# A four-layer graph network: the first stage's roots moved to ScalarE, its mask taken from bytes, its statistics summed unmerged, and an eighth of every third difference tile on GpSimd

## The chip, the core and the metric

The kernel runs on one core of a Trainium2 chip. The metric is device microseconds (us) of one execution; of several executions the median counts. The engines are PE (TensorE matmul, with PEld for its weight loads), DVE (VectorE), ACT (ScalarE), POOL (GpSimd) and SP (SyncE, which issues most DMAs here).

## The reference, cut to what matters

128 graphs of 128 nodes with 128 features pass four residual layers. The change lies in the first stage of the kernel, which computes layer 0 and the first half of layer 1:

```python
def _layernorm(x, axis=-1, eps=1e-5): ...        # (x - mean) / sqrt(var + eps)
# layer 0: relations 1 to 7; adj holds only 0 and 1 here, so one relation has edges
h = jnp.maximum(_layernorm(x), 0.0)
mask = (adj == r); degree = clip(mask.sum(axis=2), 1e-06)
agg = agg + einsum('bts,bsd->btd', mask / degree, h) @ rel_weights[r]
out = agg + h @ self_w.T + self_b
x = x + relu(layernorm(out) * ln_gamma + ln_beta)
# layer 1
h = jnp.maximum(_layernorm(x), 0.0)
D = jnp.abs(h[:, :, None, :] - h[:, None, :, :])
z = einsum('bijc,oc->bijo', D, W1) + b1           # 64 outputs for every pair i, j
m = mean(z over b, i, j); v = mean((z - m) ** 2 over b, i, j)
z = leaky((z - m) / sqrt(v + EPS) * g1 + be1)     # needs m and v of all 128 graphs
...
```

The mean and the variance of `z` over all pairs of all graphs stand between the first stage and the second.

## The kernel before, in words

There are three stages, one after the other, in one program. The first, `two_stages` up to line 755, computes layer 0 and `z`, writes `z` to memory in HBM and collects its statistics. After a short step that folds the statistics (lines 758 to 797), the second stage reads `z` back and finishes layer 1. The third computes layers 2 and 3. The change touches the first stage and the fold.

**Tiles of the first stage.** `z` is symmetric in i and j, so only half of the pairs are computed: for every graph b, 64 shifts of the node index, in 4 tiles of 2 x 8 shifts. That makes 512 tiles, numbered i = 4b + t, each 128 features by 2048 pairs. One tile passes four engines:

- `difference` (line 317): subtracts shifted features (`xe`, in SBUF) from the own ones. Tiles t = 1 and 3 (`ON_POOL`) run on GpSimd, t = 0 and 2 on VectorE, where the second operand is the copy in PSUM (`XP`). The tile t = 0 takes a maximum in place of the difference, with a correction by TensorE.
- `absolute` (line 375): ScalarE, in place, for t = 1, 2, 3.
- `products` (line 332): TensorE, 4 matmuls with `w1T` for t > 0, and 8 for t = 0.
- `evacuate` (line 345): ScalarE copies the result from PSUM into `z`, 128 x 1024.
- `statistics` (line 361): VectorE, two or three `bn_stats` for each tile. After every fourth graph `bn_aggr` (lines 372, 373) merges these into two means and variances for the group, in `ST1`.
- `kept` (line 357): SP stores `z`.

**Layer 0.** `chain(g)` (line 427) handles a group of G = 4 graphs, 32 groups in all, while the tiles of an earlier group run. Its three layer norms (of x, of layer 0's output `o`, and of the new x) each take `moments` on VectorE (lines 450, 452), and then `roots` (line 454) on GpSimd: an addition, a power of -0.5 (`rsqrt`, lines 231, 232) and `shift` (lines 289, 290), which forms -mean/deviation. ScalarE then applies them, in `centred` (line 473, four instructions of 128 x 128 for `hn`, four for `o`) and `h1` (line 514). `masked` (line 460) compares the integer adjacency with 1 on GpSimd, `degree` (464) sums it on VectorE, `shared` (477) divides on GpSimd; `m8` (537) keeps the adjacency as bytes for later layers. TensorE turns and multiplies (483 to 497), `joined` (500) adds the bias on VectorE from PSUM, `scaled` (504, 505) applies gamma and beta, `ended` (508) the relu and the residual.

**What sets the order.** Each piece of work is a `step`: a name, an engine, a cost in us, the steps that it needs, a rank. `_ranked` (line 109) plays these costs through, with one in-order queue for each engine, and always takes the step that can begin earliest; among those that begin within `NEAR` of each other, the lowest rank goes first. `RANK1` shifts the ranks by name. The result is one fixed order for each engine, written out before the program is built. `TAKEN` says which step holds one of the two PSUM tiles `sm` until which other step has read it.

A second copy of the first two stages, `two_stages(True)`, is in the program for other data; it is not executed with these inputs.

Of the kernel before, what the change touches and what calls it, by code (L numbers as in the profile page):

```python
# [17 lines left out]
P = 128  # L18
G = 4
# [11 lines left out]
ON_POOL = {1, 3}  # L31
BY_MAX = 0
# [7 lines left out]
HOPS, DEEP, ARRIVING, NEAR = 0.1, 0.25, 2.4, 0.025  # L40
LATE = {"SP": 0.0, "Pool": 0.02, "ACT": 0.1, "DVE": 0.08, "PE": 0.1}
RANK1 = {"small": 5.5, "on_all": -21, "selfb": -88.5, "both_t": 69.5, "fold": 22.5, "zero": 86.5, "xp": (25, 6.5),
         "xe": (-73.5, 2), "again": (30.5, -38), "pw": (38, -59), "xw": (84, 10.5), "load": 14, "mask": 8.5,
         "mv": 80.5, "deg": -48, "rs": -7, "most": -70, "per": 38.5, "hn": 21.5, "share": -74.5, "pt": 14,
         "hT": -24, "pm": -81.5, "maskT": 22.5, "ph": 19, "hw": 36, "m8": -10.5, "po": -82, "o": 88, "mvo": 36,
         "rso": -75.5, "oc": -23.5, "on": 62, "end": -58.5, "x": -53, "mvx": 54.5, "rsx": -54.5,
         "h1": (-13, -93.5),
         "d": (48.5, 10, -31.5, -34.5, -16.5, -63, -6, 36, 58.5, -27, -180, -50, -73.5, -31, 64, -37.5),
         "hp": (72.5, -76.5, 26, -8, 34.5, -30, -54, 43.5, 18.5, -53, 1, 6.5, -22, -157, -120, 31),
         "hs": (-114.5, -49, 10.5, -47, 55, -49, -39, -106, -123, 81, -8, -22, -42, -6.5, 17, -105),  # L50
         "st": (-5, 6.5, -4, -3.5, -137.5, -143, 69, -12.5, 117, -194.5, -100, 126, -35, -10.5, -62.5, 20.5),
         "abs": (-29.5, 55.5, -114, 8, 2, 59.5, -12.5, 6, -22, 21.5, 3.5, -62.5),
         "out0": (-10.5, -14, -143.5, 23.5), "out": (-10.5, 126, -63.5, 12.5)}
TAKEN = (("pt", "hT"), ("pm", "maskT"), ("ph", "hw"), ("po", "o"), ("on", "end"))
# [115 lines left out]
def tile_gnn_stack(ctx: ExitStack, tc: tile.TileContext, a: dict, out: bass.AP):  # L170
# [24 lines left out]
    make_identity(nc, ident)  # L195
    mhalf = const.tile([P, 1], F32, name="mhalf")
# [29 lines left out]
    ST1 = res.tile([P, NG, 2, 2], F32, name="ST1")  # L226
# [40 lines left out]
    def two_stages(general):  # L267
# [3 lines left out]
        banks = {"sm": 2}  # L271
        ahead_by = FETCHED - 2 * general

        with tc.tile_pool(name="c0", bufs=1) as c0, tc.tile_pool(name="p0", bufs=2) as p0:
# [9 lines left out]
            gamma, beta = (t[:, 2, :] for t in XP)  # L284

            def shift(mv, rs):

                nb = small.tile([P, G], F32, name="lnnb")
                nc.gpsimd.tensor_tensor(nb, mv[:, :, 0], rs, OP.mult)
                nc.gpsimd.tensor_scalar(nb, nb, -1.0, None, op0=OP.mult)  # L290
                return nb

# [8 lines left out]
            taken = [("sm", (a, g), [(b, g)]) for g in range(NG) for a, b in TAKEN] + [("sm", "on_all", ["selfb"])]  # L304

            def step(name, engine, cost, after, rank, work):
                of, n = (name, 0) if isinstance(name, str) else name[:2]
                if of in RANK1:
                    per = 16 if of in ("d", "abs", "hp", "hs", "st") else 4 if of in ("out", "out0") else \
                        2 if of in ("xp", "xe", "again", "pw", "xw") else 1  # L310
                    at = n % per - (of == "abs") * (n % per // NT + 1) if per > 1 else name[2] if of == "h1" else 0
                    rank = 16 * (n // per) + (RANK1[of][at] if isinstance(RANK1[of], tuple) else RANK1[of])
                steps.append((name, engine, cost, after, rank, 0.0, work))
# [3 lines left out]
            def difference(i):  # L317

                b, t = divmod(i, NT)
                xe, k = XE[b // 2], b % 2  # L320
                on_pool = t in ON_POOL
                d = room["d"].tile([P, 2, KC, P], F32, tag=f"d{int(on_pool)}", bufs=2 - general, name="d")
                x = xe[:, k, 0:P] if on_pool else XP[b // 2 % 2][:, k, :]
                ahead = xe[:, k, 1 + KC * t:]
                ahead = bass.AP(tensor=ahead.tensor, offset=ahead.offset,
                                ap=[list(ahead.ap[0]), [KH, 2], [1, KC], [1, P]])
                eng = nc.gpsimd if on_pool else nc.vector
                eng.tensor_tensor(d, ahead, x[:, None, None, :].to_broadcast([P, 2, KC, P]),  # L328
                                  OP.max if t == BY_MAX else OP.subtract)
                diffs[i] = d.rearrange("p h k i -> p h (k i)")  # L330

            def products(i):
                d = diffs.pop(i)
# [27 lines left out]
            def statistics(i):  # L361
# [8 lines left out]
                if last and b % G == G - 1:  # L370
                    of_all = stats.pop(b // G).rearrange("p a g b -> p a (g b)")
                    nc.vector.bn_aggr(ST1[:, b // G, 0, :], of_all[:, 0:2 * NT, :].rearrange("p a b -> p (a b)"))
                    nc.vector.bn_aggr(ST1[:, b // G, 1, :], of_all[:, 2 * NT, :])
# [4 lines left out]
            def pairs(i):  # L378
# [4 lines left out]
                step(("d", i), engine, cost, [("again", n), ("d", i - 2), ("hp", i - 4 + 2 * general)], rank, lambda: difference(i))  # L383
                if not by_max:
                    step(("abs", i), "ACT", 1.92, [("d", i)], i - 1, lambda: absolute(i))
                step(("hp", i), "PE", 3.54 if by_max else 1.82,
                     [("d" if by_max else "abs", i), ("hp", i - 1), ("hs", i - 2)] + [("xw", n)] * by_max,
# [3 lines left out]
                step(("st", i), "DVE", (1.33 if b % G < G - 1 else 2.38) if t == NT - 1 else 1.28, [("hs", i), ("st", i - 1)], i + 2,  # L391
                     lambda: statistics(i))
# [5 lines left out]
            def features(g, half):  # L398
# [3 lines left out]
                tiles = lambda m: [("d", i) for i in range(2 * NT * m, 2 * NT * m + 2 * NT)]  # L402
# [24 lines left out]
            def chain(g):  # L427
# [3 lines left out]
                t = {} if general else {"agg": selfb}  # L431
# [21 lines left out]

                def roots(last=False):
                    rs = t["rs"] = RS1[:, g] if last else small.tile([P, G], F32, name="lnrs")
                    rsqrt(rs, t["mv"][:, :, 1])
                    t["nb"] = shift(t["mv"], rs)
# [4 lines left out]
                def degree():  # L462
                    t["deg"] = small.tile([P, G], F32, name="deg")
                    nc.vector.tensor_reduce(t["deg"], t["mask"], AX.X, OP.add)
# [4 lines left out]
                def centred(dst, src, func=AF.Identity):  # L469
                    if dst not in t:  # L470
                        tile0(dst)
                    for k in range(G):
                        nc.scalar.activation(t[dst][:, k, :], t[src][:, k, :], func, bias=t["nb"][:, k:k + 1],
                                             scale=t["rs"][:, k:k + 1])

                def shared():
                    nc.gpsimd.tensor_tensor(t["mask"], t["mask"], t["deg"][:, :, None].to_broadcast([P, G, P]),
                                            OP.mult)
# [14 lines left out]
                def gathered():  # L493
                    po = t["po"] = sm("po")
                    for k in range(G):
                        nc.tensor.matmul(po[:, k, :], t["hT"][:, k, :], both[:, 1, :], start=True, stop=False)
                        nc.tensor.matmul(po[:, k, :], t["maskT"][:, k, :], t["hw"][:, k, :], start=False, stop=True)

                def joined():
                    nc.vector.tensor_tensor(tile0("o"), t["po"], t["agg"], OP.add)  # L500

                def scaled():
                    t["on"] = sm("on")
                    nc.vector.tensor_tensor(t["o"], t["o"], over_group(gamma), OP.mult)
                    nc.vector.tensor_tensor(t["on"], t["o"], over_group(beta), OP.add)

                def ended():
                    nc.vector.scalar_tensor_tensor(t["x"], t["on"], 0.0, t["x"], op0=OP.max, op1=OP.add)
# [13 lines left out]
                step(("mask", g), "Pool", 1.51, begun, s0 + 1, masked)  # L522
                step(("mv", g), "DVE", 1.13, begun, s0 + 3, lambda: moments("x"))
                step(("deg", g), "DVE", 0.67, own("mask"), s0 + 3.1, degree)
                step(("rs", g), "Pool", 1.92, own("mv"), s0 + 5, roots)
                step(("most", g), "Pool", 0.25, own("deg"), s0 + 5.1, at_least)
                step(("per", g), "DVE", 0.15, own("most"), s0 + 7, lambda: nc.vector.reciprocal(t["deg"], t["deg"]))
                step(("hn", g), "ACT", 1.62, own("rs"), s0 + 7, lambda: centred("hn", "x", AF.Relu))
                step(("share", g), "Pool", 1.04, own("per"), s0 + 9, shared)
                step(("pt", g), "PE", 0.65, own("hn"), s0 + 9, lambda: turned("hn"))  # L530
                step(("hT", g), "ACT", 0.6, own("pt"), s0 + 9.5, lambda: copied("hT", "pt"))
# [6 lines left out]
                step(("po", g), "PE", 2.2, own("maskT", "hw"), s0 + 14, gathered)  # L538
                step(("o", g), "DVE", 0.68, own("po", "agg") + ["selfb"], s0 + 15, joined)
                step(("mvo", g), "DVE", 1.13, own("o"), s0 + 15.1, lambda: moments("o"))  # L540
                step(("rso", g), "Pool", 1.92, own("mvo", "hn"), s0 + 17, roots)
                step(("oc", g), "ACT", 1.62, own("rso"), s0 + 18, lambda: centred("o", "o"))
                step(("on", g), "DVE", 1.39, own("oc") + ["on_all"], s0 + 20, scaled)
# [3 lines left out]
                step(("rsx", g), "Pool", 1.92, own("mvx", "oc", "m8"), s0 + 23, lambda: roots(True))  # L547
# [1190 lines left out]
```

## Time and profile before

| what | value |
|---|---|
| median of 3 runs | 2649.07 us (2648.42 to 2656.91) |
| the profiled execution's own time | 2653.83 us |
| its span, first to last instruction | 2652.0 us |
| mean granted TensorE clock | 0.985 |
| first stage, until the last statistics | about 1453 us |
| second stage | about 1459 to 2250 us |
| busy over the whole span: PE, DVE, ACT, POOL | 2425, 2469, 2377, 1694 us |
| 500 to 900 us: DVE, ACT, PE, POOL busy | 399.1, 394.3, 385.6, 382.8 of 400 us |

A row of groups gives line, engine, operation, what is written from what, shapes, count, then busy time, the mean duration of one in ns, and the engine's idle time just before them with what ended it. Consecutive instructions of one engine overlap in the records, so that means times counts come to more than the time in which they ran; the distance from start to start, read in the timeline, is what an instruction takes from its engine. The lines of 40 digits show the busy share of 40 equal slices in tenths.

### The profile page before, as it was taken

The numbers are of one execution on the slowest core, as the hardware profiler recorded it, in microseconds if no ns is written. First come the engines' busy times: TensorE is split into PE (matmuls) and PEld (weight loads), VectorE is DVE, ScalarE is ACT, GpSimd is POOL, SyncE is SP. The second block draws the span as 40 slices with busy tenths as digits, with TensorE's granted clock in tenths as the row PEclk, the third lists the DMA queues.
The fourth block names the chain that finished last, engine by engine and source line by source line (L and its number), as shares of the span: only waits on it lengthen the run. The fifth ranks groups of instructions, "written<-read, shape, count | busy, mean of one in ns | idle before, by whom it ended". The sixth has DMA issues, their size and how long they took to land. (4 is left out here: it accounts for less than half of the span.)

```text
span 2652.0 us, 41948 instructions
## 1 busy us (share of the span) xinstructions
PE 2425.3 (91%) x14521; PEld 1155.4 (44%) x14521; DVE 2468.8 (93%) x4740; ACT 2376.6 (90%) x2821; POOL 1693.7 (64%) x1628
## 2 busy tenths in 40 slices
PE   6999999999999999999998988888888887999997
PEld 3333333333333333333332444444444445777776
DVE  5999999999999999999998898888888897899997
ACT  5999999999999999999998978887777774999997
POOL 6999999999999999999996110101110014666663
PEclk8999999999999999999999999999999997999999
DMA  3555555555555555555556899999999982021211
GB/s 102 199 207 210 209 212 207 214 208 211 207 210 207 210 207 210 207 210 210 207 210 227 339 408 410 409 410 409 410 409 410 398 345 81 21 69 57 66 36 34
DMA packets 185426, 611.43 MB, mean 231 GB/s; under 512 B 31987, under 2 KB 99702, under 8 KB 121718
## 3 DMA queue, kind: packets, MB, share of 16 engines
q1 hardware_dynamic: 184768, 608.50, 59.8%
q8 instruction: 118, 1.93, 0.3%
q14 instruction: 102, 0.84, 0.1%
q10 hardware_dynamic: 438, 0.17, 0.0%
HBM read 312.58 MB, written 296.03 MB: 229 GB/s over the span
## 5 line engine op out<-in xcount | busy, mean ns | idle before, releaser
L328 POOL TENSOR_TENSOR d<-xe 128x2048 f32<-128x2048 f32 x256 | 1073.5, 4203 | 36.5 <-PE hp L338 34.5
L338 PE MATMUL hp<-d,w1T 128*64 128x512 f32 x4096 | 994.2, 601 | 57.0 <-ACT z L352 54.0
L376 ACT ACTIVATE d<-d 128x2048 f32<-128x2048 f32 x384 | 733.5, 1922 | 20.2 <-POOL d L328 19.8
L328 DVE TENSOR_TENSOR d<-xe,xp 128x2048 f32<-128x2048 f32 x256 | 580.1, 2266 | 6.9 <-POOL xe L423 4.0
L352 ACT COPY z<-hp 128x1024 f32<-128x1024 f32 x512 | 519.0, 1015 | 9.7 <-PE hp L338 4.6
L338 PEld LDWEIGHTS hp<-d,w1T 128*64 128x64 f32 x4096 | 277.2, 136 | 558.7 <-issue 454.7
L997 POOL TENSOR_TENSOR x<-x,bt 128x512 f32<-128x512 f32 x27 | 39.1, 1449 | 555.6 <-DMA x<-x 447.7
L366 DVE BATCH_NORM_STATS2 st<-z 128x6 f32<-128x512 f32 x512 | 347.6, 679 | 6.1 <-ACT z L352 6.0
L367 DVE BATCH_NORM_STATS2 st<-z 128x6 f32<-128x512 f32 (+1 forms) x512 | 329.2, 643 | 0.0
L945 DVE SCALAR_TENSOR_TENSOR z<-z 128x2048 f32<-128x2048 f32 x128 | 297.8, 2327 | 6.3 <-ACT z L915 6.3
L926 ACT ACTIVATE zr<-z,bias,scale 128x2048 f32<-128x2048 f32 x128 | 267.3, 2089 | 7.8 <-DVE bias L797 7.8
L915 ACT ACTIVATE z<-z,bias,scale 128x2048 f32<-128x2048 f32 x128 | 267.0, 2087 | 0.0
L341 PE MATMUL hp<-both_t,xw 128*64 128x512 f32 x1024 | 265.2, 592 | 0.0
L892 PE MATMUL ps<-z,w2z 128*32 128x512 f32 x1024 | 139.5, 616 | 65.1 <-DVE z L945 64.8
L899 PEld LDWEIGHTS pk<-pick,su 128*128 128x128 f32 x1024 | 124.0, 191 | 138.1 <-DVE su L913 105.9
L899 PE MATMUL pk<-pick,su 128*128 128x16 f32 x1024 | 136.4, 265 | 25.5 <-DVE su L913 24.9
L892 PE MATMUL ps<-z,w2l 128*32 128x512 f32 x1024 | 139.7, 607 | 2.1 <-DVE w2l L853 2.1
L341 PEld LDWEIGHTS hp<-both_t,xw 128*64 128x64 f32 x1024 | 77.6, 137 | 142.1 <-issue 142.1
L892 PE MATMUL ps<-zr,w2r 128*32 128x512 f32 x1024 | 139.0, 608 | 0.0
L1629 PE MATMUL pv<-wr,e 128*128 128x128 f32 x1024 | 134.0, 278 | 2.0 <-ACT wr L1554 1.1
L1629 PEld LDWEIGHTS pv<-wr,e 128*128 128x128 f32 x1024 | 124.1, 192 | 8.3 <-ACT wr L1554 1.7
L1606 DVE SCALAR_TENSOR_TENSOR e<-e,ps 128x512 f32<-128x512 f32 x160 | 106.7, 674 | 10.7 <-ACT ps L1603 10.3
(257 smaller groups left out, 3788.7 us busy)
## 6 DMA issues: line engine op xcount, KB each, us to landing
hp<-z SPq DMA_DIRECT2D x248, 1024.0 KB, 4.0
z<-hp SPq DMA_DIRECT2D x248, 1024.0 KB, 13.0
x<-x SPq DMA_DIRECT2D x118, 256.0 KB, 5.4
u<-rows SPq DMA_DIRECT2D x32, 384.0 KB, 11.5
x<-in_x_dram SPq DMA_DIRECT2D x32, 256.0 KB, 5.6
adj<-in_adj_dram SPq DMA_DIRECT2D x32, 256.0 KB, 5.9
z<-y SPq DMA_DIRECT2D x27, 256.0 KB, 11.8
y<-z SPq DMA_DIRECT2D x27, 256.0 KB, 2.8
```

What stands on the lines that cost most here:

```text
L328: eng.tensor_tensor(d, ahead, x[:, None, None, :].to_broadcast([P, 2, KC, P]), OP.max if t == BY_MAX else OP.subtract)
L338: nc.tensor.matmul(hp[64 * hh:64 * hh + 64, c:c + 512], w1T2 if by_max else w1T, d[:, hh, c:c + 512], start=True, stop=not by_max, skip_gr ...
L341: nc.tensor.matmul(hp[64 * hh:64 * hh + 64, c:c + 512], XW[i // NT // 2][:, i // NT % 2, :], both_t.rearrange("p h k i -> p h (k i)")[:, h ...
L352: nc.scalar.copy(half_of(b, t), linear.pop(i))
L366: nc.vector.bn_stats(st[:, 2 * t, :], hs[:, 0:512])
L367: nc.vector.bn_stats(st[:, 2 * t + 1, :], hs[:, 512:1024 - P * last])
L376: nc.scalar.activation(diffs[i], diffs[i], AF.Abs)
L892: nc.tensor.matmul(ps[32 * c:32 * c + 32, :], w[:, w0:w0 + 32], v[:, 512 * c:512 * c + 512], start=start, stop=stop, skip_group_check=True)
L899: nc.tensor.matmul(pk[:, kk, 0:16], su[:, kk, :], pick.rearrange("p h j -> p (h j)"), start=True, stop=True)
L915: linear = lambda z: nc.scalar.activation(z, z, AF.Identity, bias=bias1, scale=scale1[:, 0:1])
L926: nc.scalar.activation(zr, z1, AF.Relu, bias=bias1, scale=scale1[:, 0:1])
L945: nc.vector.scalar_tensor_tensor(z0, z0, 0.01, z0, op0=OP.mult, op1=OP.max)
```

## The change

All of it is in the first stage and the fold behind it; the second and third stages keep their code.

- **Roots.** `roots` on GpSimd becomes `deviation` (ScalarE, square root of variance + eps), `roots` (VectorE, reciprocal) and, where a shift is needed, `shift` (GpSimd, two small instructions as before). The three layer norms of a group each get the first two; the one of `o` needs no shift.
- **Mask from bytes.** `masked` goes. `degree` sums the byte tile `M8[g]`, and `shared` multiplies its four parts by the degree's reciprocal into `mask`.
- **`hn`.** ScalarE normalises three of the four graphs, GpSimd the fourth; the relu of that one moves into the copy `hT`.
- **Layer 0's output** stays in PSUM. A matmul of three bf16 parts of the bias starts the accumulation, so `joined` and `oc` go, and `scaled` becomes eight `scalar_tensor_tensor` of 128 x 128 that apply mean and gamma, then deviation and beta. `po` is held until `ended`.
- **Shared difference tile.** Of the tile t = 2, shifts 0 to 6 of 8 are computed on VectorE, shift 7 on GpSimd (2 x 128 columns).
- **Statistics.** The two `bn_aggr` of a group go. Per group, ScalarE squares the means less a reference mean in place (128 x 72), and GpSimd adds the whole tile (128 x 216) to a running sum. The fold then weighs that sum once.
- **Order.** All of `RANK1` has new values, and `NEAR` goes from 0.025 to 0.055.

```diff
-HOPS, DEEP, ARRIVING, NEAR = 0.1, 0.25, 2.4, 0.025
+HOPS, DEEP, ARRIVING, NEAR = 0.1, 0.25, 2.4, 0.055
+SHARED, ITS_K = 2, 7
-TAKEN = (("pt", "hT"), ("pm", "maskT"), ("ph", "hw"), ("po", "o"), ("on", "end"))
+TAKEN = (("pt", "hT"), ("pm", "maskT"), ("ph", "hw"), ("po", "end"))
...
-                if last and b % G == G - 1:
-                    of_all = stats.pop(b // G).rearrange("p a g b -> p a (g b)")
-                    nc.vector.bn_aggr(ST1[:, b // G, 0, :], of_all[:, 0:2 * NT, :].rearrange("p a b -> p (a b)"))
-                    nc.vector.bn_aggr(ST1[:, b // G, 1, :], of_all[:, 2 * NT, :])
+            def squared(g):
+                nc.scalar.activation(of_group(g)[:, :, 0], of_group(g)[:, :, 1], AF.Square, bias=less1)
+            def added_up(g):
+                total = ST1.rearrange("p a b f -> p (a b f)")
+                nc.gpsimd.tensor_tensor(total, total, stats.pop(g).rearrange("p a g f -> p (a g f)"), OP.add)
...
+                if t == SHARED:
+                    step(("dp", i), "Pool", 0.59, free, rank, lambda: difference(i, slice(ITS_K, KC), True))
+                    step(("d", i), engine, 2.01, free, rank, lambda: difference(i, slice(0, ITS_K)))
...
+                def deviation():
+                    t["sd"] = small.tile([P, G], F32, name="lnsd")
+                    nc.scalar.activation(t["sd"], t["mv"][:, :, 1], AF.Sqrt, bias=eps_c)
                 def roots(last=False):
                     rs = t["rs"] = RS1[:, g] if last else small.tile([P, G], F32, name="lnrs")
-                    rsqrt(rs, t["mv"][:, :, 1])
-                    t["nb"] = shift(t["mv"], rs)
+                    nc.vector.reciprocal(rs, t["sd"])
...
-                    nc.vector.tensor_reduce(t["deg"], t["mask"], AX.X, OP.add)
+                    nc.vector.tensor_reduce(t["deg"], t["mask"] if general else M8[g], AX.X, OP.add)
...
+                    for k in range(G):
+                        nc.gpsimd.tensor_scalar(t["mask"][:, k, :], src[:, k, :], t["deg"][:, k:k + 1], None, op0=OP.mult)
...
+                        nc.tensor.matmul(po, ones3, s_parts[:, None, :].to_broadcast([3, G, P]), start=True,
+                                         stop=False, skip_group_check=True)
...
-                    nc.vector.tensor_tensor(t["o"], t["o"], over_group(gamma), OP.mult)
-                    nc.vector.tensor_tensor(t["on"], t["o"], over_group(beta), OP.add)
+                    for k in range(G):
+                        nc.vector.scalar_tensor_tensor(t["o"][:, k, :], po[:, k, :], t["mv"][:, k, 0:1], gamma,
+                                                       op0=OP.subtract, op1=OP.mult)
+                    for k in range(G):
+                        nc.vector.scalar_tensor_tensor(po[:, k, :], t["o"][:, k, :], t["rs"][:, k:k + 1], beta,
+                                                       op0=OP.mult, op1=OP.add)
...
-                step(("mask", g), "Pool", 1.51, begun, s0 + 1, masked)
-                step(("rs", g), "Pool", 1.92, own("mv"), s0 + 5, roots)
+                step(("sd", g), "ACT", 0.32, own("mv"), s0 + 4, deviation)
+                step(("rs", g), "DVE", 0.15, own("sd"), s0 + 5, roots)
+                step(("nb", g), "Pool", 0.46, own("rs"), s0 + 6, shift)
-                step(("hn", g), "ACT", 1.62, own("rs"), s0 + 7, lambda: centred("hn", "x", AF.Relu))
-                step(("share", g), "Pool", 1.04, own("per"), s0 + 9, shared)
+                step(("hn", g), "ACT", 1.24, own("nb"), s0 + 7, centred)
+                step(("hn3", g), "Pool", 0.54, own("hn"), s0 + 7, lambda: centred((G - 1,)))
+                step(("share", g), "Pool", 1.9, own("per"), s0 + 9, shared)
...
-                step(("oc", g), "ACT", 1.62, own("rso"), s0 + 18, lambda: centred("o", "o"))
-                step(("on", g), "DVE", 1.39, own("oc") + ["on_all"], s0 + 20, scaled)
+                step(("on", g), "DVE", 1.75, own("rso") + ["on_all"], s0 + 20, scaled)
```

## The prediction

> **What bounds the kernel now.** I read the busy shares by slice first, then the engines' busy times in a quiet stretch, then the groups of instructions there, and last the timeline of one group of four graphs.
>
> ```profile
> DVE  5999999999999999999998898888888897899997
> ACT  5999999999999999999998978887777774999997
> DMA  3555555555555555555556899999999982021211
> ```
>
> The first 22 slices are the first stage: VectorE and ScalarE full, DMA at half. Next 500 to 900 us (columns: PE, PEld, DVE, ACT, POOL with counts, clock, DMA share, GB/s):
>
> ```profile
> 500.00:900.00 400.00, 385.58 (x1850) 145.96 (x1847) 399.06 (x688) 394.34 (x426) 382.75 (x238) 1.00 0.56 210
> ```
>
> All four engines are at 96% or more, so one engine's relief is worth only the distance to the next. The prices, from 200 to 1300 us, 25 groups:
>
> ```profile
> L328 POOL TENSOR_TENSOR d<-xe 128x2048 f32<-128x2048 f32 x200 | 838.6, 4203 | 20.1 <-PE hp L338 19.8 <-issue 0.3
> L328 DVE TENSOR_TENSOR d<-xe,xp 128x2048 f32<-128x2048 f32 x200 | 453.0, 2265 | 0.0
> L232 POOL TENSOR_TENSOR lnrs<-lnrs,mhalf 128x4 f32<-128x4 f32 x50 | 51.8, 1036 | 4.2
> L473 ACT ACTIVATE o<-o,lnnb,lnrs 128x128 f32<-128x128 f32 x100 | 41.4, 493 | 0.0
> L460 POOL TENSOR_SCALAR mask<-adj 128x512 f32<-128x512 int32 x25 | 37.6, 1506 | 0.0
> L372 DVE BATCH_NORM_AGGREGATE ST<-st 128x2 f32<-128x192 f32 x25 | 25.1, 1004 | 0.0
> ```
>
> VectorE idles nowhere. Durations overlap, so I price by the distance between starts. VectorE's timeline:
>
> ```profile
> 801.64 0.68 DVE L464 TENSOR_REDUCE deg<-mask 128x4 f32<-128x512 f32 x1
> ...
> 803.49 1.00 DVE L372 BATCH_NORM_AGGREGATE ST<-st 128x2 f32<-128x192 f32 x1
> 804.41 0.20 DVE L373 BATCH_NORM_AGGREGATE ST<-st 128x2 f32<-128x24 f32 x1
> 804.53 2.23 DVE L328 TENSOR_TENSOR d<-xe,xp 128x2048 f32<-128x2048 f32 x1
> ...
> 845.77 0.68 DVE L464 TENSOR_REDUCE deg<-mask 128x4 f32<-128x512 f32 x1
> ```
>
> From `deg` to `deg` a group lasts 44.13 us, and VectorE works through it start to start: **VectorE 44.13, with no slack**. In the same group ScalarE shows one wait of 0.47 us and some gaps of 0.05 to 0.1 us: it needs about 43.3. GpSimd shows waits of 0.17 and 0.61: 43.4, counting the gaps inside its root chains. TensorE shows waits of 0.87, 0.18 and 0.42: at most 42.7. Its uninterrupted pace is 0.215 us a record, 34.3 for the 160 records of the tiles, plus 6.2 for the rest: at least 40.5. One root chain on GpSimd:
>
> ```profile
> 810.05 0.23 POOL L231 TENSOR_SCALAR RS<-MV 128x4 f32<-128x4 f32 x1
> 810.36 1.04 POOL L232 TENSOR_TENSOR RS<-RS,mhalf 128x4 f32<-128x4 f32 x1
> 811.47 0.20 POOL L289 TENSOR_TENSOR lnnb<-MV,RS 128x4 f32<-128x4 f32 x1
> 811.76 0.24 POOL L290 TENSOR_SCALAR lnnb<-lnnb 128x4 f32<-128x4 f32 x1
> ```
>
> The two root instructions hold GpSimd 1.42 us (0.08 to 0.1 of it twice as a gap between dependent ones), the shift 0.50 to the next start at 811.97.
>
> [...]
> - [...] the trace has one load, 1.28 us, at the start.
> - [...] No run here shows sqrt. In the built order of the changed kernel one load stands before the first sqrt and one before the first exp[...].
> - [...] The trace's 128-column `bn_stats` from SBUF takes 0.20 from start to start (803.29 to 803.49).
> [...]
>
> **The change part by part**, per group, from start to start.
>
> *Statistics.* VectorE loses the merges, 803.49 to 804.53: -1.04. [...] GpSimd the sum of 216 columns: 0.44 at 2.05 ns, 0.65 at 2.83 (the `x` plus `bt` row at line 997, 1449 ns for 512) plus little; I take 0.58. Nobody waits for these but the buffer of statistics two groups on.
>
> *Shared tile, four a group.* [...] GpSimd: 256 columns, 0.52 at the row's slope, 0.67 if line 595's 0.32 us for 64 columns is mostly fixed; I take 0.59, +2.36. `abs` of that tile now waits for both.
>
> *Roots, three a group.* GpSimd -3 x 1.42 - 0.50 = -4.76. [...] VectorE +3 x 0.08 (the reciprocal at 816.91 let the next begin at 816.99) = 0.24; up to 0.16 each if it is waited for. Behind each reciprocal stand VectorE's statistics and differences; in the new order 1.2 us of statistics lie between the moments of `o` and the next reciprocal, while ScalarE may be inside an `abs` (1.81). Bounds of this wait: 0 to 1.8 a group; I count it in the 0.4 below.
>
> *Layer 0's output.* VectorE: `joined` -0.59 (828.39 to 828.98); `scaled` was 839.23 to 840.60, -1.37, and is now 8 x 0.20 = 1.60 [...]. ScalarE: `oc` -1.56 (836.22 to 837.78). TensorE: one bf16 matmul of 512 columns, +0.22 by the record's pace, up to 0.4. `po` holds a PSUM tile some 10 us instead of 3; the other one serves the transposes, whose producers have the rest of the 44 us.
>
> *hn.* ScalarE: a quarter of 1.54 (831.09 to 832.63), -0.38. GpSimd +0.5 (fixed 0.24, 128 columns at the 1.6 to 2.5 ns of lines 995 and 460).
>
> *Mask.* GpSimd -1.48 for `masked` and -0.99 for `shared`; four parts of 128 columns, 0.44 each (fixed 0.23, then line 995's 1.6 ns from bytes), +1.75; at line 460's slope 0.6, 2.4. The byte sum on VectorE as before, 0.59.
>
> Sums:
> - VectorE -1.04 - 1.07 + 0.24 - 0.59 - 1.37 + 1.60 = -2.23: 41.9 [...].
> - ScalarE 0.25 + 0.57 - 1.56 - 0.38 = -1.12: **42.2**.
> - GpSimd 0.58 + 2.36 - 4.76 + 0.5 - 2.47 + 1.75 = -2.04: 41.4 (to 42.6 with the dear ends).
> - TensorE +0.22: 40.7 to 42.9.
>
> So VectorE stops being alone at the end: ScalarE is late next, 0.3 above VectorE and under the upper value of TensorE. Before, the full engine had no waits at all; with two or three equally full I add 0.4: **42.6 a group, -1.53**. Steady running lasts from the first difference (38.8 us) to about 1440: 31.7 groups, **-48.5 us**. The new ranks have no price of their own: they decide how much of the 0.4 to 1.5 is lost.
>
> *Start.* Group 0's chain runs alone, so its latency counts in full:
>
> ```profile
> 21.09 0.23 POOL L231 TENSOR_SCALAR lnrs<-lnmv 128x4 f32<-128x4 f32 x1 [10.39 <-DVE lnmv L452]
> 23.09 1.65 ACT L473 ACTIVATE o<-o,lnnb,lnrs 128x128 f32<-128x128 f32 x4 [6.92 <-POOL lnnb L290]
> 38.77 4.49 DVE L328 TENSOR_TENSOR d<-xe,xp 128x2048 f32<-128x2048 f32 x2 [4.03 <-POOL xe L423]
> ```
>
> The middle root, 2.0 us, becomes about 0.7; `oc` (1.65) and `joined` (0.7) go; the last root loses 0.8; the first, which waited for the mask on GpSimd, 1.6; `scaled` gains 0.3. Together -5.8: **-6** (-3 to -9).
>
> *Fold.* The merges (1.05) give way to square and sum (1.0 with hops); behind them the second pass gets shorter by some 0.5. **-0.5.** Later stages: a table load before the first exp (1512 us). ScalarE waits there for VectorE, 1.65 us on average, so part is hidden: **+1** [...]. ScalarE's queue issues seven small DMAs at the start instead of six (gamma now goes to all partitions, the bias comes three times more); the six end at 4.2 us, and an issue of some 0.4 more still ends before the first root is ready at about 5: 0.
>
> Sum: -48.5 - 6 - 0.5 + 1 = -54. The profiled execution took 2653.8 us (span 2652.0), which gives 2600; it lies 4.8 above the median, so against the median 2649.1 the forecast is **2595 us**.
>
> **The rivals.**
> - *The handshakes eat half (0.13).* A reciprocal that waits 0.5 to 1 us for ScalarE, or TensorE at its upper 42.9 plus waits: 43.5 a group, -0.63 x 31.7 - 5 = -25: 2624. For it: ScalarE's queue is full of 1.8 us pieces. Against: such moments lie among much other work on VectorE.
> - *GpSimd becomes the bound (0.10).* At the dear ends it needs 42.6, and it showed 0.8 of waits for TensorE's buffers: 43.4, -0.73 x 31.7 - 5 = -28: 2621.
> - *Slower: the joint (0.06).* Each group has four tiles whose `abs` needs GpSimd's small part, queued in order behind a 4.2 us difference. ScalarE has 44.13 - 42.6 plus 0.2 from the start = 1.7 us a group to lose: above 0.43 us for each joint the change turns slower. At 0.65: 45.2, +1.07 x 31.7 - 5 = +29: 2678. Against: the plan knows both parts.
> - *Table loads at every root (0.01).* Six loads a group, 7.7 us: about 2840. The built order speaks against it.
> - *Better than counted (0.05).* ScalarE overlaps more than I grant, 41.7: 2566. *No difference (0.03).*
>
> **How the numbers follow.** My case has 0.62; within it 42.2 to 43.1 a group gives 2582 to 2611. Two measurements of this kernel can tell 0.3% from no change, 8 us. Faster by more: 0.62 + 0.13 + 0.10 + 0.05 = 0.90; same 0.03; slower 0.07. The range, 2574 to 2632, leaves out most of the better case, the slower ones and no difference, 0.15 in all, and some of the tails.
>
> **What would show it.** From `deg` to `deg` some 42.6 us; no root on GpSimd in the first stage; ScalarE's idle time below 0.5 us a group; first difference near 33 us; eight 128-column instructions of about 0.27 us duration for `scaled`; GpSimd's small part near 0.6. It is wrong if ScalarE waits for GpSimd before `abs` by half a microsecond a tile, if VectorE idles before the reciprocals, or if more than two table loads appear.

## The result and the profile after

| what | before | after |
|---|---|---|
| median of 6 runs each | 2652.6 us (2648.42 to 2656.91) | 2637.62 us (2629.52 to 2638.2) |
| ratio, 95% interval | | 0.9938 (0.992 to 0.9957) |
| span of the profiled execution | 2652.0 us | 2635.9 us |

The kernel became faster by about 15 us, where 54 were forecast. Its time lies above the range's upper end of 2632. I take the two spans apart, 16.1 us, at four marks that both traces have:

| stretch | before | after | difference | forecast |
|---|---|---|---|---|
| start to first difference on VectorE | 38.77 | 36.29 | -2.5 | -6 |
| from there to the start of the last `bn_stats` | 1413.4 | 1397.6 | -15.8 | -48.5 |
| from there to the bias, the end of the fold | 6.64 | 6.39 | -0.2 | -0.5 |
| second and third stage | 1193.2 | 1195.6 | +2.4 | +1 |

Of the 38 us that are missing, 33 are missing in the long second stretch (48.5 - 15.8), that is in every group of four graphs. The engine rows of the page of the kernel after, slice by slice, still look as before:

```profile
DVE  6999999999999999999997898889888896899997
ACT  5999999999999999999998977787788774999996
...
DMA  3555555555555555655555999999999982022201
```

The busy times in a stretch of the first stage tell more (columns: us, PE, PEld, DVE, ACT, POOL with counts, clock, DMA share, GB/s):

```profile
500.00:900.00 400.00, 391.24 (x1888) 144.86 (x1884) 392.13 (x751) 390.05 (x422) 382.75 (x240) 1.00 0.56 212
```

VectorE went from 399.1 to 392.1 of 400 us: it is no longer full. But no engine is full now, and all four stand at 96 to 98%. The time from `deg` to `deg` is in the row of that instruction in the kernel after (count, durations in ns, first and last start):

```profile
L491 DVE TENSOR_REDUCE deg<-m x22: 660/666/673, 316.8 to 1233.7; 128x4 f32<-128x512 uint8 x22
```

22 starts bound 21 groups: (1233.7 - 316.8) / 21 = **43.66 us**. Before it was 44.14 (21 starts from 316.2 to 1198.9), so a group gained 0.48 us and not the 1.53 forecast. 0.48 x 31.7 groups = 15.

The groups of instructions of the kernel after, 200 to 1300 us, put prices beside the estimates (busy us, mean ns | idle before them and what ended it):

```profile
L328 POOL TENSOR_TENSOR d<-xe 128x2048 f32<-128x2048 f32 x203 | 852.9, 4208 | 27.0 <-PE hp L337 17.3 <-ACT hT L520 9.7
...
L328 POOL TENSOR_TENSOR d<-xe 128x256 f32<-128x256 f32 x101 | 75.3, 746 | 0.0
L512 POOL TENSOR_SCALAR mask<-m,deg 128x128 f32<-128x128 uint8 x100 | 59.5, 617 | 0.0
...
L548 DVE SCALAR_TENSOR_TENSOR po<-o,lnrs,xp 128x128 f32<-128x128 f32 x101 | 35.9, 356 | 3.6
...
L545 DVE SCALAR_TENSOR_TENSOR o<-po,lnmv,gamma 128x128 f32<-128x128 f32 x104 | 28.5, 336 | 0.0
...
L475 ACT ACTIVATE lnsd<-lnmv,eps_c 128x4 f32<-128x4 f32 x52 | 14.9, 289 | 2.1
```

The small part of a shared tile takes GpSimd 746 ns, not 590, and a part of `shared` 617, not 440. On VectorE the eight instructions of `scaled` take 336 and 356 ns, not about 270. Who waits now, in the same stretch of the kernel after (us in total, times, longest):

```profile
ACT d L384 <- POOL d L328: 25.4, 73, 0.8
PE hp L337 <- ACT z L351: 21.6, 50, 0.7
...
POOL d L328 <- PE hp L337: 17.3, 50, 0.5
DVE st L365 <- ACT z L351: 16.8, 25, 0.9
POOL xe L442 <- ACT xe L429: 14.8, 25, 0.6
```

Read as arrows these lines close a circle: ScalarE waits for GpSimd's differences (1.0 us a group), GpSimd for the buffers that TensorE gives back (0.7), TensorE for the PSUM that ScalarE empties (0.9). GpSimd also waits for ScalarE directly, for a copy into `xe` (0.6). VectorE waits too, but in the whole list only a weight load (PEld) waits for VectorE, in a stretch where TensorE itself shows no wait for it. So VectorE's work seems to lie outside the circle. GpSimd's timeline in the kernel after shows one arc, and the second fence what ScalarE does beside it:

```profile
799.86 4.90 POOL L328 TENSOR_TENSOR d<-xe 128x2048 f32<-128x2048 f32 x2 [0.17 <-PE hp L337]
804.74 2.38 POOL L512 TENSOR_SCALAR mask<-m,deg 128x128 f32<-128x128 uint8 x4
807.08 0.66 POOL L381 TENSOR_TENSOR ST<-ST,st 128x216 f32<-128x216 f32 x1
807.68 8.37 POOL L328 TENSOR_TENSOR d<-xe 128x2048 f32<-128x2048 f32 x2
...
816.81 4.91 POOL L328 TENSOR_TENSOR d<-xe 128x256 f32<-128x256 f32 x2
```

```profile
811.93 1.91 ACT L384 ACTIVATE d<-d 128x2048 f32<-128x2048 f32 x1 [0.33 <-POOL d L328]
...
816.08 1.91 ACT L384 ACTIVATE d<-d 128x2048 f32<-128x2048 f32 x1 [0.50 <-POOL d L328]
...
818.79 1.91 ACT L384 ACTIVATE d<-d 128x2048 f32<-128x2048 f32 x1
...
821.75 1.91 ACT L384 ACTIVATE d<-d 128x2048 f32<-128x2048 f32 x1 [0.15 <-POOL d L328]
```

From 799.86 to 821.7 GpSimd works without a pause, and the four parts of `shared` and the statistics stand in the middle of its differences. ScalarE takes three of these differences the moment they end: 811.93 is the end of the first of the two that began at 807.68. The waits in brackets add up to 0.98 us. All three are for whole tiles of GpSimd (t = 3, 1, 3). The `abs` at 818.79 is that of a shared tile, whose small part was made from 816.81 on, and it waits for nothing. From 200 to 1300 us all 73 waits before `abs` are of this kind, none is at a shared tile: the small parts are ready in time, but they, `shared` and the sum push back the whole tiles behind them.

### The profile page after: what moved, and what is told of

Its sections match the earlier page's. It is cut to its first block, busy times and chain, and to the rows that moved or that the text cites. A ratio compares the mean times of both kernels' runs of the same rounds, so it can differ in the third digit from the quotient of the medians.

```text
span 2635.9 us, 42291 instructions
## 1 busy us (share of the span) xinstructions
PE 2431.0 (92%) x14549; PEld 1140.3 (43%) x14549; DVE 2435.7 (92%) x4938; ACT 2347.3 (89%) x2789; POOL 1682.0 (64%) x1639
## 3 DMA queue, kind: packets, MB, share of 16 engines
q8 instruction: 118, 1.93, 0.3%
## 5 line engine op out<-in xcount | busy, mean ns | idle before, releaser
L328 POOL TENSOR_TENSOR d<-xe 128x2048 f32<-128x2048 f32 (+1 forms) x384 | 1164.4, 3054 | 39.0 <-PE hp L337 27.3
L328 DVE TENSOR_TENSOR d<-xe,xp 128x2048 f32<-128x2048 f32 (+1 forms) x256 | 546.4, 2135 | 3.8 <-POOL xe L442 1.6
L337 PEld LDWEIGHTS hp<-d,w1T 128*64 128x64 f32 x4096 | 262.8, 136 | 544.0 <-issue 376.9
```

The source lines that it names most:

```text
L337: nc.tensor.matmul(hp[64 * hh:64 * hh + 64, c:c + 512], w1T2 if by_max else w1T, d[:, hh, c:c + 512], start=True, stop=not by_max, skip_gr ...
```

## The experiments

The theory after this reading, **A**: the circle through GpSimd's small parts and ScalarE sets the pace. The rivals: **B**, VectorE does, whose `scaled` costs 1 us a group more than counted; **C**, TensorE does, which got a matmul more. The first four kernels each take work from one engine and keep the written order of every engine.

**Half of `scaled` left out** (VectorE):

```diff
-                        nc.vector.scalar_tensor_tensor(t["o"][:, k, :], po[:, k, :], t["mv"][:, k, 0:1], gamma,
+                        nc.vector.scalar_tensor_tensor(po[:, k, :], po[:, k, :], t["mv"][:, k, 0:1], gamma,
                                                        op0=OP.subtract, op1=OP.mult)
-                    for k in range(G):
-                        nc.vector.scalar_tensor_tensor(po[:, k, :], t["o"][:, k, :], t["rs"][:, k:k + 1], beta,
-                                                       op0=OP.mult, op1=OP.add)
```

> Leaves out the second four of the eight instructions of scaled (deviation and beta); every engine's order stays. VectorE has 1.43 us a group less to do. Theory A, a ring through GpSimd's small parts and ScalarE sets the pace and VectorE has 0.65 us to spare: the group stays at 43.6 (43.5 to 43.7), the time within 4 us of 2637. Theory B, VectorE's dearer scaled sets the pace: the group falls to 43.0 or below, 2617 or less. Theory C, TensorE at its upper need of 42.8 sets it: no difference.

Measured: 43.67 us a group, 2634.99 us, ratio to before 0.9923 (0.9907 to 0.994). The four instructions that stay now write PSUM and take 1.42 us where the eight took 2.57, so VectorE was relieved of 1.15 us a group, not of 1.43. It became idle and nothing else changed, as the row of this kernel from 500 to 900 us shows beside the one above:

```profile
500.00:900.00 400.00, 391.26 (x1888) 144.75 (x1884) 384.20 (x724) 389.96 (x422) 382.75 (x238) 1.00 0.56 213
```

VectorE is busy for eight us less in 400, ScalarE, TensorE and GpSimd are equal to 0.1, and the group did not follow. Theory B falls.

**`shared` as one copy** (GpSimd):

```diff
-                    for k in range(G):
-                        nc.gpsimd.tensor_scalar(t["mask"][:, k, :], src[:, k, :], t["deg"][:, k:k + 1], None, op0=OP.mult)
+                    nc.gpsimd.tensor_scalar(t["mask"], src, 1.0, None, op0=OP.mult)
```

> The four byte multiplications of a group on GpSimd become one copy of 128 x 512; leaves out the division by the degree; every engine's order stays. GpSimd has 1.3 us a group less. Theory A: the group falls to about 43.0, where VectorE is full, 2617. Theories B and C: 43.6, 2634 to 2638.

Measured: 43.08 us a group, 2621.34 us, 0.9873 (0.9856 to 0.9889). The copy took 1507 ns in place of 2.38 us: 0.88 us less on GpSimd gave 0.58 less a group.

**The self-weight matmuls left out** (TensorE):

```diff
-                        nc.tensor.matmul(po[:, k, :], t["hT"][:, k, :], both[:, 1, :], start=general, stop=False,
-                                         skip_group_check=True)
```

> Leaves out the four matmuls of the self weights; every engine's order stays. TensorE has 0.9 us a group less. Theory C: the group falls by 0.5 or more, 2620 or less. Theories A and B: by 0.2 at most, 2630 to 2638.

Measured: 43.67 us a group, 2634.41 us, 0.9928 (0.9912 to 0.9945). Theory C falls: 0.9 us less on TensorE changes nothing but TensorE's own waits for ScalarE, which grow from 21.6 to 36.3 us between 200 and 1300 us.

**`hn` of three graphs as one relu** (ScalarE):

```diff
-                        nc.scalar.activation(t["hn"][:, k, :], t["x"][:, k, :], AF.Relu, bias=t["nb"][:, k:k + 1],
-                                             scale=t["rs"][:, k:k + 1])
+                        if k == 0:
+                            nc.scalar.activation(t["hn"][:, 0:3, :], t["x"][:, 0:3, :], AF.Relu)
```

> The three normalisations of hn on ScalarE become one relu of 128 x 384; leaves out mean and deviation of these three graphs; every engine's order stays. ScalarE has 0.67 us a group less. Theory A: the group falls by 0.5 to 0.65, to about 43.0, 2617. Theories B and C: by 0.2 at most, 2630 to 2638.

Measured: 43.31 us a group, 2624.57 us, 0.9889 (0.9873 to 0.9906). ScalarE took 0.43 us for the relu in place of 1.17 for the three, 0.74 less (not 0.67), and this gave 0.35 less. So work taken from GpSimd or ScalarE shortens the group, work taken from VectorE or TensorE does not: theory A stands. TensorE is a link in the list of waits all the same. To stand in that list is not enough for an engine's work to count; it takes a kernel with less of that work to tell.

**A second operation for `shared`.** The copy of 512 columns took 2.9 ns a column and the four parts 4.8. GpSimd's other `tensor_scalar` with two operations (`hn`, line 501) takes 447 ns for 128 columns, less than the 617 of `shared` with one. So I gave `shared` a second operation that adds zero, which leaves the result the same:

```diff
-                        nc.gpsimd.tensor_scalar(t["mask"][:, k, :], src[:, k, :], t["deg"][:, k:k + 1], None, op0=OP.mult)
+                        nc.gpsimd.tensor_scalar(t["mask"][:, k, :], src[:, k, :], t["deg"][:, k:k + 1], 0.0, op0=OP.mult,
+                                                op1=OP.add)
```

> Computes what the changed kernel does; the four byte multiplications on GpSimd get a second operation, the addition of 0. In the changed kernel 128 columns take 617 ns there with one operation, and 447 ns with two (the fourth graph of hn). If the one-operation form is what is dear, GpSimd gains 0.68 us a group and the ring theory wants 43.1 to 43.2 a group, about 2621 us. If bytes are what is dear, 0.6 us each, 43.66 and 2637 stay.

The group of this kernel, to be read beside the 617 above:

```profile
L512 POOL TENSOR_SCALAR mask<-m,deg 128x128 f32<-128x128 uint8 x100 | 35.5, 375 | 0.0
```

Measured: 375 ns each, 43.09 us a group, 2619.12 us, 0.9877 (0.9861 to 0.9894). With it GpSimd's new work costs what the prediction had counted: 4 x 0.70 for the small parts, 1.38 for `shared`, 0.60 and 0.41 for the sum and `hn`, from start to start, make 5.19, against 5.19 (0.58 + 2.36 + 0.5 + 1.75). The waits of this kernel:

```profile
POOL d L328 <- PE hp L337: 38.9, 101, 0.8
...
ACT lnsd L475 <- DVE lnmv L471: 13.6, 26, 0.5
PE hp L337 <- ACT z L351: 10.2, 26, 0.4
```

ScalarE's waits for GpSimd are gone (0.2 us in all). In their place it waits 0.5 us a group for VectorE's moments before a root. This kernel took 0.96 us a group from GpSimd and the copy 0.88, yet they end at 43.09 and 43.08: beyond that, another limit holds, and less work on GpSimd buys nothing more.

**The bias parts later** (start). In the kernel after, VectorE's first work is the splitting of the bias into three bf16 parts, and the first moments stand behind it:

```profile
5.70 0.21 DVE L636 CAST one<-left 3x128 bf16<-3x128 f32 x1 [4.71 <-DMA left<-in_self_b_dram]
...
8.43 0.85 DVE L469 BATCH_NORM_STATS2 lnst<-x 128x6 f32<-128x128 f32 x4
...
36.29 4.22 DVE L328 TENSOR_TENSOR d<-xe,xp 128x2048 f32<-128x2048 f32 x2 [1.65 <-POOL xe L442]
```

```diff
-                step("parts", "DVE", 1.7, ["small"], -20, in_parts)
+                step("parts", "DVE", 1.7, ["small", ("mv", 0), ("deg", 0), "both_t"], -20, in_parts)
```

> Computes what the changed kernel does; the nine small instructions that split the bias stand behind the first moments on VectorE instead of ahead of them. If they hold up the start, the first moments come at 3.8 us instead of 8.4, and the first difference at 32 to 33 us instead of 36.3; the group stays at 43.66, the time falls by about 3.5 us. If the first chain is bound elsewhere, the first difference stays at 36.

VectorE's timeline in this kernel, whose second line is the first difference:

```profile
3.70 0.87 DVE L469 BATCH_NORM_STATS2 lnst<-x 128x6 f32<-128x128 f32 x4 [2.70 <-DMA x<-in_x_dram]
...
32.46 2.29 DVE L328 TENSOR_TENSOR d<-xe,xp 128x2048 f32<-128x2048 f32 x1 [1.63 <-PE pt L517]
```

Measured: the first difference begins at 32.46 in place of 36.29, the group is unchanged at 43.65; 2632.29 us, 0.9915 (0.9899 to 0.9932). That interval overlaps the one of the kernel after, so it is the traces that show the effect: in the three kernels with the late bias parts the first difference begins at 30.2 to 32.5 us, in all others with the new code at 34.8 to 36.8.

**The ranks and `NEAR` of before** in the code of after; steps that are new have no shift:

```diff
-HOPS, DEEP, ARRIVING, NEAR = 0.1, 0.25, 2.4, 0.055
+HOPS, DEEP, ARRIVING, NEAR = 0.1, 0.25, 2.4, 0.025
...
-RANK1 = {"small": -768.5, "on_all": 411.5, "parts": 557.5, ...
+RANK1 = {"small": 5.5, "on_all": -21, "selfb": -88.5, "both_t": 69.5, ...
```

> Computes what the changed kernel does, in the order that the ranks and NEAR of the kernel before give. If the new order is what makes the lighter engines pay, a group takes 44.2 us or more and the time is 2655 or more. If the order is of little weight, 43.7 and 2639.

Measured: 2844.27 us, 1.0711 (1.0694 to 1.0729), 49.9 us a group. Its waits from 200 to 1300 us:

```profile
POOL d L325 <- PE hp L334: 149.8, 107, 4.7
...
DVE st L362 <- ACT z L348: 92.4, 77, 3.6
PE hp L334 <- ACT d L381: 92.0, 36, 6.1
```

Single waits of 4 to 6 us: the same instructions in another order cost 6.2 us a group. The granted clock was 0.96 there, 1.00 in the same stretch of the kernel after; TensorE's busy time from 500 to 900 us grew only from 42.7 to 43.8 us a group, so the clock is not the main cause.

**The tile t = 2 whole on VectorE**, the order kept:

```diff
-                    step(("dp", i), "Pool", 0.59, free, rank, lambda: difference(i, slice(ITS_K, KC), True))
-                    step(("d", i), engine, 2.01, free, rank, lambda: difference(i, slice(0, ITS_K)))
+                    step(("dp", i), "Pool", 0.59, free, rank, lambda: None)
+                    step(("d", i), engine, 2.01, free, rank, lambda: difference(i))
```

> Computes what the changed kernel does; VectorE does the whole tile t = 2, GpSimd's part goes, and every engine's order stays. VectorE needs 43.0 + 1.07 = 44.1, GpSimd 2.8 less. If VectorE's need is read rightly, a group takes 44.1 us, 2651. If GpSimd alone sets the pace, the group falls below 43.2 and the time below 2623.

Measured: 43.96 us a group, 2645.9 us, 0.9969 (0.9959 to 0.9978). VectorE is full again:

```profile
500.00:900.00 400.00, 388.63 (x1865) 142.90 (x1867) 398.72 (x745) 386.52 (x422) 355.41 (x203) 1.00 0.56 210
```

With VectorE full, 43.96 is its need, and less the 1.07 us that were moved back to it (four tiles, which take 1.92 us each from start to start in the kernel after where a whole one takes 2.19) this makes **42.89** for the kernel after. The prediction had 41.9. Moving the eighth to GpSimd was thus worth 0.30 us a group, although GpSimd paid 2.8 us for the 1.07.

**Both cheap edits and `scaled` to SBUF.** The second four instructions of `scaled` write SBUF, where they promised to be shorter, and `ended` reads them there; with the two edits before:

```diff
-                        nc.vector.scalar_tensor_tensor(po[:, k, :], t["o"][:, k, :], t["rs"][:, k:k + 1], beta,
+                        nc.vector.scalar_tensor_tensor(t["o"][:, k, :], t["o"][:, k, :], t["rs"][:, k:k + 1], beta,
...
-                    nc.vector.scalar_tensor_tensor(t["x"], t["po"], 0.0, t["x"], op0=OP.max, op1=OP.add)
+                    nc.vector.scalar_tensor_tensor(t["x"], t["o"], 0.0, t["x"], op0=OP.max, op1=OP.add)
```

> Computes what the changed kernel does, with three edits: the two-operation byte multiplication of e5, the late bias split of e6, and the second four of scaled writing to SBUF instead of PSUM (VectorE some 0.3 us a group less, if writing to PSUM is what makes them 0.36 us each against 0.28). VectorE is full at 43.08 in e5, so a group should take about 42.8, and the first difference come at about 32: 2619 - 9 - 4 = 2606. If the ring through GpSimd is not loosened below 43.08, 43.08 and 2615[...].

Measured: slower than before, 2690.2 us, 1.0138 (1.0114 to 1.0161), 45.61 a group. `scaled` did get shorter (1.03 us for the four, not 1.43), but `ended` now has two inputs in SBUF. Its group, then the instruction in VectorE's timeline, then GpSimd's timeline beside it, all of this kernel:

```profile
L553 DVE SCALAR_TENSOR_TENSOR x<-o,x 128x512 f32<-128x512 f32 x24 | 93.8, 3909 | 0.0
```

```profile
721.90 3.92 DVE L553 SCALAR_TENSOR_TENSOR x<-o,x 128x512 f32<-128x512 f32 x1
```

```profile
720.38 4.89 POOL L328 TENSOR_TENSOR d<-xe 128x256 f32<-128x256 f32 x2
```

3909 ns in place of 674, and all 24 of them from 200 to 1300 us took 3896 to 3925. The instruction ends at 725.82, 0.55 us after GpSimd's pair at 725.27. The same instruction of the first group, at 22.27 us and so ahead of the first difference, took 0.69 us. By these times it seems to wait until GpSimd is done, and nothing in the lists of waits says so, since the record counts this time as busy. GpSimd's whole differences took 4204 ns here, 4208 in the kernel after: they did not get longer.

**The second operation, with half of `scaled` left out**, to see whether VectorE is the pace at 43.09 (the edits of the two kernels that are named so above, together):

> e5 with the second four instructions of scaled left out (deviation and beta); every engine's order stays. VectorE has 1.43 us a group less than in e5. If VectorE alone is the bound of e5 at 43.08, the group falls to the ring's own pace, between 42.6 (43.66 less the whole 0.97 that GpSimd gained) and 42.8, 2605 to 2611. If the ring already sets the pace again at 43.08, no difference from e5, 2619.

Measured: 43.09 us a group again, 2616.55 us, 0.9866 (0.9846 to 0.9887). VectorE is not the pace there. (Here too the four that stay write PSUM: it was relieved of 1.15 us.)

**The two edits that leave out nothing**, second operation and later bias parts:

> Computes what the changed kernel does: the two-operation byte multiplication of e5 with the late bias split of e6, and nothing else. A group of 43.09 as in e5, the first difference 3 us earlier than in e5's 35.2: 2619 - 3 = 2616. If the late split disturbs the steady order, more than 43.2 a group.

Measured: 2612.91 us (2609.04 to 2616.17), ratio to before 0.9844 (0.983 to 0.9859), 43.10 us a group, first difference at 30.16. It computes what the kernel after computes, and is the fastest kernel here that leaves nothing out.

**The second operation, with TensorE or ScalarE relieved** (the self-weight matmuls left out; `hn` as one relu):

> e5 with the four matmuls of the self weights left out; every engine's order stays. TensorE has 0.9 us a group less. If the 43.09 of e5 is a ring in which TensorE is the full engine (42.7 of need by its waits), the group falls to 42.7 or below, 2606 or less. If ScalarE is the full one, 43.0 to 43.1, 2617.

> e5 with the three normalisations of hn on ScalarE made one relu (mean and deviation of these three graphs left out); every engine's order stays. ScalarE has 0.67 us a group less. If ScalarE is the full engine of e5's ring, the group falls to 42.4 to 42.7, 2598 to 2607. If TensorE is, 43.0 to 43.1, 2617.

Measured: 42.89 us a group in both; 2614.46 us, 0.9843 (0.9826 to 0.986), and 2611.89 us, 0.9839 (0.9824 to 0.9854). The busy row of the second of them from 240 to 1180 us shows where this stops:

```profile
240.00:1180.00 940.00, 927.87 (x4496) 346.71 (x4497) 936.87 (x1801) 912.80 (x966) 893.40 (x573) 1.00 0.57 215
```

VectorE is at 936.9 of 940 us, the rest being a gap of 0.14 us a group inside `scaled`: it is full at 42.89, the need that the unshared tile had given.

## Why the prediction was wrong

Right were the sign, the place (nearly all of the gain lies in the groups of the first stage), the statement that VectorE would no longer be alone at the end, and some small terms. The wait before a reciprocal, which the prediction bounded at 0 to 1.8 us, does not appear in the list of waits of the kernel after.

- *Table load:* +1 was forecast, an estimate of mine that no trace of before shows. It is one `ACT_TABLE_LOAD` of 1.28 us at 1492.6, the only one besides that of the start, with ScalarE busy before and after it. That the second stage grew by 1.3 us and the third by 1.1, from 429.2 to 430.3, proves nothing for or against the forecast: with the same code behind the fold, the two stages together took from 1188 to 1199 us in the traces of this study's kernels.
- *Roots:* the square root of 4 columns takes 289 ns, 357 for the third norm. From start to start the three hold ScalarE for 0.89 us a group (twice 0.32, once 0.25), where the prediction's sum has 0.57; the square of 72 columns holds it for 0.29, where the sum has 0.25. Both terms were estimates of mine that no trace of before shows. The reciprocals take 0.08 from start to start. No root is left on GpSimd.
- *Fold:* -0.2 instead of -0.5.

Wrong were these steps.

**1. GpSimd's dear ends ("GpSimd ... 41.4 (to 42.6 with the dear ends)").** I took 0.59 for the small part and 0.44 for a part of `shared`, from slopes of other rows. They cost 0.70 and 0.59 from start to start: +0.4 and +0.6 a group, -0.1 for `hn`. What followed is that ScalarE waits for GpSimd before `abs`, 1.0 us a group. It is not the rival "joint": no `abs` of a shared tile waits, the waits are for whole tiles that come late. Nor is GpSimd full: in the kernel after it still waits 1.7 us a group itself (17.3, 9.7 and 14.8 us in 25 groups). A prediction that compares the engines' sums cannot see this; what counts is how late a single difference is. The kernel with the second operation, where GpSimd's sum is the predicted one, measures what this term is worth: 43.66 - 43.09 = **0.57 us a group, 18 us in all**. Of the rivals, "GpSimd becomes the bound" (43.4, 2621; chance 0.10) named the engine; in its number "the handshakes" (43.5, 2624; 0.13) came nearest, but the wait before a reciprocal that it built on did not appear.

**2. "With two or three equally full I add 0.4."** Even with GpSimd as cheap as predicted, and VectorE 0.2 below its predicted need (42.89 - 1.15 = 41.74), the group takes 43.09 and not 42.6. ScalarE's own work is 42.4 to 42.6 (its busy time for each group from 240 to 1180 us, with the second operation and in the kernel after), 0.2 to 0.4 above the predicted 42.2. The rest is waits, 0.7 us a group on ScalarE alone, where 0.4 was allowed: 0.5 for the moments before a root, 0.2 for a matmul. So this step is worth **0.49 us a group, 16 us**. Relieving TensorE or ScalarE brings 0.2 of it, down to 42.89, where VectorE is full. Which links close this second circle is not settled, since relieving either works and since the moments that ScalarE waits for did not come earlier when VectorE had less to do. Nor was it tried whether another order would loosen it: the written order was reckoned with 0.59 for a small part and 1.9 for `shared`, not with what they take.

**3. `scaled`: "8 x 0.20 = 1.60".** From 818.41 to 820.98 it takes 2.57 in the kernel after: 1.14 for the four that write SBUF, 1.43 for the four that write PSUM. The 0.20 is the distance of another instruction in the trace of before, a `bn_stats` of 128 columns. An instruction of `scaled` that writes SBUF begins 0.26 us after the one before it. One that writes PSUM begins 0.39 us after the one before it, and that the estimate left out. This term explains VectorE's need to the last tenth (41.9 + 0.97 = 42.87 against 42.89). But it cost nothing here: leaving half of it out changed neither 43.66 nor 43.09. It only stops what else could be gained at 42.89.

**4. The start, -6.** The chain got shorter as counted, but I did not look at what the new step `parts` stands ahead of. It waits for a DMA until 5.70, and the first moments, which could begin at 3.70 in the kernel with the late parts, followed it at 8.43. With `parts` moved the first difference begins at 32.46, -6.3 against before: the term was right, and a step put ahead of it took 3.8 us of it between these two traces.

**5. "The new ranks have no price of their own: they decide how much of the 0.4 to 1.5 is lost."** With the ranks of before the same instructions take 49.9 us a group. An order can decide over 6 us, not 1; that it was good in the kernel after could not be read from the profile before. How much of the missing gain a still better order would bring was not tried, so this step has no share in the sum below.

The sum closes: 1.06 us (0.57 + 0.49) x 31.7 = 33.6 us, the start 3.5, the later stages 1.4 (which lies within the scatter named above) and the fold 0.3 make 39; 54 - 16 = 38 were missing.

## What to carry to other kernels

When several engines stand at 96 to 98% and none is full, look for a circle of waits and not for a fullest engine: list who waits for whom, then take work from one engine after the other. Here less work on GpSimd or ScalarE bought 0.47 to 0.66 us for each us, down to the next limit, and less work on TensorE nothing, though it stood in the list. Price a small instruction on GpSimd from a row of its own size and form, not by a slope from large ones: of the 746 ns for 256 columns a third is a fixed part (an estimate from these and the 4208 ns for 2048), and one form took 617 ns where another took 375. And when a step is added at the start of a queue, ask what was first there before.

## What the runs showed of the hardware that was not expected

- GpSimd's `tensor_scalar` from bytes to f32, 128 x 128, took 617 ns with one operation and 375 ns with two. With one operation and a constant factor 128 x 512 took 1507 ns.
- A two-input difference on GpSimd took 746 ns for 256 columns and 4208 for 2048. By these two rows a column takes 1.93 ns and the fixed part is 0.25 us, an estimate; the 2.05 ns a column of the row for 2048 alone would make it 0.53 us for 256.
- A VectorE instruction with two SBUF inputs, 128 x 512, took 3909 ns (24 of them, 3896 to 3925), instead of 674 with one of them in PSUM. The one at 721.90 us ran beside a 4.2 us difference of GpSimd and ended 0.55 us after it; the one of the first group, ahead of the first difference, took 0.69 us.
- `scalar_tensor_tensor` of 128 columns on VectorE: one that writes SBUF began 0.26 us after the one before it, one that writes PSUM 0.39 us. All eight into SBUF took 2.04 us (712.10 to 714.14 in the kernel whose `scaled` writes SBUF alone), four and four 2.57.
